# Layer 0 of a graph network: results turned over in pieces of four transposes, and the LSTM's output product cut in two

## The chip, the cores and the metric

The kernel runs on one NeuronCore of a Trainium2 chip. The metric is device time in microseconds (us), the median of several runs. One execution was also taken by the hardware profiler; its trace gives the start, length, tiles and releaser of each instruction. The engines are TensorE (PE; its weight loads are listed apart as PEld), VectorE (DVE), ScalarE (ACT), GpSimd (POOL) and SyncE (SP), which here only issues DMAs.

## The reference, cut to what matters

The input x holds 128 graphs of 64 nodes with 256 features, or 8192 tokens. Four layers follow one another, each x = x + f(relu(layernorm(x))). Layers 1 to 3 are an edge-softmax attention, a graph convolution with batch norms and a dense attention. The change lies in layer 0, with its last pieces of work in the first steps of layer 1:

```python
h = relu(einsum('ts,bsh->bth', adj, x @ Wg0 + bg0))
h = relu(einsum('ts,bsh->bth', adj, h @ Wg1 + bg1))
for p in range(1, 5):
    nw = 64 // p
    wins = h[:, :nw * p].reshape(128 * nw, p, 256)
    last = lstm_last(Wih[p-1], Whh[p-1], bih[p-1] + bhh[p-1], wins)
    h = h.at[:, arange(nw) * p + p - 1].set(last.reshape(128, nw, 256))
```

The LSTM starts from zero. At each of its p steps the gates i, f, g and o come from x_t @ Wih.T + h @ Whh.T + bias; then c = sigmoid(f)*c + sigmoid(i)*tanh(g) and h = sigmoid(o)*tanh(c). The last h overwrites the p-th node of each window, and the next p reads what the previous one left. All is in fp32.

## The kernel before, in words

**Where the data is.** The tokens are cut into 16 chunks of 512 and 4 groups of 2048. The features of a group lie transposed (256 features as 2 x 128 partitions, tokens along the free axis) in a tile hT. Only two such tiles fit, so the stage works in two halves: first groups 0 and 1, then groups 2 and 3. The features of groups 2 and 3 wait in device memory (hm8 to hm15) until a result of the first half has left hT.

**Steps.** A Step (L671) is one time step t of one window length w for one part of a group: 512 tokens wide for w=1, 256 for w=2, 336 for w=3, 256 for w=4. Each half runs w=1 to 4; the parts go in pairs whose steps alternate, so a state's next step comes a whole step of the other state later. Step.prepare (L693) makes the operand tile xop from hT: for w=1 by DVE (L704, L708 and the next), for larger w by copies L715 and L716 and subtractions L717, L723 and L724, on ACT and DVE, or on GpSimd where the first step of the other state stands beside it.

**Products.** The 256-deep product of a gate is done with seven products of 128x128 blocks, after Strassen and Winograd (L734 for all of them). Step.gate (L769) is a generator in four parts: products 1 and 2 (into PSUM tiles pa and pb; copy L777, add L778); products 6 and 7 (copies L782, L785); product 5 (add L788); products 3 and 4 (add L793), after which gate_done runs. The values of a gate lie in a tile of four blocks, numbered 0 to 3. Blocks 0 and 2 have feature half 0, blocks 1 and 3 half 1. Two activations (func, L762) finish the halves in the last part: the one of half 0 after product 3, the one of half 1 after product 4's add.

**gate_done** (L797) makes c (L811 to L814) and tanh(c) (L815). After gate o it makes the result: in the last step one product o*tanh(c) written straight into hT (L828), in earlier steps one product into a tile lstm_h (L833), and behind it three differences (L835 to L837) that the next step's products need. For w=1 it is two products per feature half (L820).

**The order is written by hand.** The loop over slots begins one gate per slot and keeps three in flight: the new gate's products 1 and 2, the oldest gate's 3 and 4 with gate_done, the middle gate's 5, the new gate's 6 and 7. At the end of the slot come the outputs that are due, preparing of the next step, loads of residuals (fetch_x, L855), and weights of later phases (L494, with sums on GpSimd at L506). Engines take their instructions in this order.

**PSUM.** In this stage the tag "bank" has two buffers. Product 2's pb and the transposes of results share them.

**Outputs.** group_out(g, c) (L862) returns chunk column c of a finished group: for each u of two, chunk n = 4g+2u+c, it calls add_transposed twice. Each call is four 128x128 transposes (L188) into one bank and one DVE add (L193) of the bank to the residual tile xres. After both calls GpSimd issues the store of xres to xa (L869). In the first half SP then issues the load (L872) that fills the freed columns of hT with those of the second half. A group is put out by two calls of 16 transposes, one slot and then three slots after its last step (two in the second half). xres has four buffers; loads for the next group stand later on SP's queue and wait for those stores. The last group's calls come in layer 1, one in each of the first two calls of edges (L1409); layer 1 has transposes of its own (L173), and adds L1070.

Of the kernel before, what the change touches and what calls it, by code (L numbers as in the profile page):

```python
# [31 lines left out]
def gnn_stack_kernel(ctx: ExitStack, tc: tile.TileContext, a: dict, out: bass.AP):  # L32
# [446 lines left out]
    with ExitStack() as l0:  # L479
# [191 lines left out]
        class Step:  # L671
# [97 lines left out]
            def gate(self, q):  # L769

                N = self.N
                pa = psl.tile([P, 512], F32, tag="pa", name="pa", bufs=3)
                pb = psl.tile([P, 512], F32, tag="bank", name="pb", bufs=2)
                pc = psl.tile([P, 512], F32, tag="pc", name="pc", bufs=3)
                self.product(q, ((1, pa, True), (2, pb, True)))
                blk, second = self.new_gate(q)
                nc.scalar.copy(blk[0, 0], pa[:, :N])  # L777
                nc.vector.tensor_tensor(blk[0, 0], pb[:, :N], blk[0, 0], ALU.add)  # L778
                self.func(q, blk[0, 0], blk[0, 0], 0)
                yield  # L780
                self.product(q, ((6, pa, False),))
                nc.scalar.copy(blk[1, 0], pa[:, :N])  # L782
                self.product(q, ((7, pc, True),))

                (nc.vector.tensor_copy if not self.t and self.w > 1 else nc.scalar.copy)(blk[1, 1], pc[:, :N])  # L785
                yield
                self.product(q, ((5, pa, False),))
                nc.vector.tensor_tensor(blk[1, 1], pa[:, :N], blk[1, 1], ALU.add)  # L788
                yield
                self.product(q, ((3, pa, False),))  # L790
                self.func(q, blk[0, 1], pa[:, :N], 0)
                self.product(q, ((4, pc, False),))
                nc.vector.tensor_tensor(blk[1, 0], pc[:, :N], blk[1, 0], ALU.add)  # L793
                self.func(q, second, second, 1)
                self.gate_done(q)

            def gate_done(self, q):  # L797
                N, state, t = self.N, self.state, self.t
                last = t == self.w - 1
                act = self.act  # L800
                if q == 2 and t:
                    for i_, g_ in zip(act[0], act[2]):
                        nc.vector.tensor_tensor(i_, i_, g_, ALU.mult)
                if (q == 1) if t else (q == 2):
                    if not t and self.w > 1:
                        state["c"] = [cp.tile([P, 4 * NMAX], F32, tag="c", name="lstm_c")[:, : 4 * N]]
                    for k in range(len(act[0])):
                        i_, g_ = act[0][k], act[2][k]
                        c_ = state["c"][k] if self.w > 1 else i_
                        if t:  # L810
                            nc.vector.tensor_tensor(act[1][k], act[1][k], c_, ALU.mult)  # L811
                            nc.vector.tensor_tensor(c_, act[1][k], i_, ALU.add)
                        else:
                            nc.vector.tensor_tensor(c_, i_, g_, ALU.mult)  # L814
                        nc.scalar.activation(g_, c_, AF.Tanh)  # L815
                if q != 3:
                    return
                if self.w == 1:
                    for j in range(2):
                        nc.vector.tensor_tensor(  # L820
                            self.nodes(slice(j, j + 3, 2), 0),
                            act[3][j].rearrange("p (u n) -> p u n", n=N),
                            act[2][j].rearrange("p (u n) -> p u n", n=N),
                            ALU.mult,
                        )
                elif last:
                    o_, g_ = (act[k][0].rearrange("p (q n) -> p q n", n=N) for k in (3, 2))
                    nc.vector.tensor_tensor(  # L828
                        self.nodes(slice(0, 4), t), self.as_nodes(o_), self.as_nodes(g_), ALU.mult
                    )  # L830
                else:
                    h = hop.tile([P, 7 * NMAX], F32, tag="h", name="lstm_h")
                    nc.vector.tensor_tensor(h[:, : 4 * N], act[3][0], act[2][0], ALU.mult)  # L833
                    v = h[:, : 7 * N].rearrange("p (q n) -> p q n", n=N)
                    nc.vector.tensor_tensor(v[:, 4:6], v[:, 2:4], v[:, 0:3:2], ALU.subtract)  # L835
                    nc.vector.tensor_tensor(v[:, 6], v[:, 3], v[:, 4], ALU.subtract)
                    nc.vector.tensor_tensor(v[:, 2], v[:, 1], v[:, 6], ALU.subtract)  # L837
                    state["h"] = {1: v[:, 0], 2: v[:, 1], 3: v[:, 3], 4: v[:, 2], 5: v[:, 4], 6: v[:, 6], 7: v[:, 5]}
# [20 lines left out]

        residual = {}  # L860

        def group_out(g, c):  # L862

            for u in range(2):
                n = 4 * g + 2 * u + c
                xt = residual.pop(n)
                for ip in range(2):
                    add_transposed(xt, 2 * ip, hTs0[g % 2][:, u], c * CHUNK + ip * 256)
                nc.gpsimd.dma_start(out=xa[n], in_=xt)  # L869
                if g < 2:  # L870
                    m = n + NCH // 2
                    nc.sync.dma_start(  # L872
                        out=hTs0[g][:, u, :, c * CHUNK : (c + 1) * CHUNK], in_=hmem[m]
                    )

        def first_norms1(norms):

# [25 lines left out]
        for slot in range(len(tasks) + 2):  # L903
# [13 lines left out]
            if len(flight) > 1:  # L917
                old = flight.pop(0)
                next(old[1], None)
                next(flight[-1][1])  # L920
            elif flight and not new:
                old = flight.pop(0)
                next(old[1], None)
            else:
                old = None
                if flight:
                    next(flight[-1][1])
            if new:
                next(one)
                flight.append((new, one))  # L930
                at, k = new[0], new[2]
                while outs and outs[0][0] <= slot:
                    group_out(*outs.pop(0)[1:])

                new_half = at + 1 < len(steps) and at and steps[at + 1].w == 1 < step.w
                if k == len(step.gates) - (1 if new_half else 2) and at + 1 < len(steps):
                    steps[at + 1].prepare(step)
                if step.w == MAX_SKIP and step.t == 2 and k < 2 and step.g < NGR - 1:
                    for u in range(2):
                        n = 4 * step.g + 2 * u + k  # L940
                        later.append((slot, "x", n))
# [7 lines left out]
            if old:  # L949
                (at, q, k), step = old[0], steps[old[0][0]]  # L950
                if k == len(step.gates) - 1:
                    if at + 1 == len(steps) or steps[at + 1].phase != step.phase:
                        phase_over(step.phase)
                    if step.phase == len(phases) - 1 and step.t == 1 and step.g == NGR - 1:

                        t_ = wsp.tile([P, 2, 4, 2, P], F32, tag="wih", name="x_first", bufs=2)
                        flat = t_.rearrange("p k q j m -> p k (q j m)")
                        norms1 = {}
                        for n in range(2):
                            xt = flat[:, n, :].rearrange("p (i d) -> p i d", i=4)  # L960
                            nc.sync.dma_start(out=xt, in_=xa[n])
                            norms1[n] = Norm(xt)
                        norm_steps = first_norms1(norms1)
                    if step.w == MAX_SKIP and step.t == MAX_SKIP - 1:
                        outs += [(slot + 1, step.g, 0), (slot + (3 if step.g < NGR // 2 else 2), step.g, 1)]
        last_outs = [(g, c) for _, g, c in outs]
    psums["banks"] = None


# [1 line left out]
    with ExitStack() as l1:  # L971
# [29 lines left out]
        nc.sync.dma_start(out=wlv[:, :, QS:], in_=a["W_valT"])  # L1001
        wout = w1.tile([P, 2, D], F32, tag="wout", name="wout")
        nc.sync.dma_start(out=wout, in_=a["W_outT"])
        for g, c in last_outs:
            for u in range(2):
                n = 4 * g + 2 * u + c
                residual[n] = fetch_x(n)

# [393 lines left out]
        def next_score():  # L1402
            q, lrs = waiting.pop(0)
            score(q, lrs)
            if q % 8 == 7:
                linear_part(q // 8)
                behind.append(edge_softmax(q // 8))

        def edges(q):  # L1409

            n, odd = q // 2, q % 2
            it = 2 * q
            halves = gather(it)
            if it + 2 < NT:
                project(it + 2)
            lrs = [joined(halves)]
# [5 lines left out]
            elif n + 2 < NCH:  # L1422
                for k in (2, 3):
                    norms1[n + 2].placed(k)
            if last_outs:
                group_out(*last_outs.pop(0))
            step_behind()
            halves = gather(it + 1)
            if it + 3 < NT:
                project(it + 3)  # L1430
            lrs.append(joined(halves))
# [784 lines left out]
```

## Time and profile before

| what | us |
|---|---|
| median of 3 runs | 1985.58 (1983.38 to 1989.72) |
| the profiled execution, its own time | 1985.91 |
| its span in the profile | 1984.1 |
| TensorE busy in it | 1938.8 |
| LSTM stage, about 190 to 1265: TensorE busy of 1075 | 1059.8 |
| the same: DVE, ACT, GpSimd busy | 643.7, 627.4, 146.5 |
| layer 1, about 1265 to 1540: TensorE busy of 275 | 265.1 |

The mean granted TensorE clock is 0.997 of full speed. A row of the timeline gives start, duration, engine, line, operation, tiles out<-in, shape, count, and in brackets the idle time ahead of it with what ended it. A row of the waits gives the engine, the tile and line that waited, what it waited for, and then us in total, times, and the longest. SPq is SP's queue of DMA issues. In the timeline the second half of the LSTM stage begins at about 700.

### The profile page before, as it was taken

What the parts mean: (1) busy time and instruction counts of PE and PEld (TensorE: products, weight loads), DVE (VectorE), ACT (ScalarE), POOL (GpSimd) and SP (SyncE); (2) the same over time, 40 slices, a digit from 0 to 9 for tenths busy, and PEclk for the clock granted to TensorE, in tenths of its full rate; (3) what the DMA queues carried; (4) which work ended last, traced back from release to release, by engine and by line L of the source; (5) the groups of instructions that cost most, each with busy time, mean ns of one, the idle gap of its engine ahead of it and who ended that gap; (6) DMA issues with size and microseconds to landing.
All of it is one profiled execution on the core that took longest, in us unless ns stands there. A gap on an engine that the chain in (4) does not pass through costs nothing. (4 is left out here: it accounts for less than half of the span.)

```text
span 1984.1 us, 25549 instructions
## 1 busy us (share of the span) xinstructions
PE 1938.8 (98%) x9406; PEld 1392.2 (70%) x9406; DVE 1309.4 (66%) x2454; ACT 1143.5 (58%) x2153; POOL 448.0 (23%) x590
## 2 busy tenths in 40 slices
PE   9999999999999999999999999999999999999998
PEld 7777478866678864788666788766556675534787
DVE  8774675575475557765654655657657777796886
ACT  4343775565465547665654656466666556593554
POOL 3000032030030011320300200255664430000574
PEclk9999999999999999999999999999999999999999
DMA  7522000010010054000100100441332842022112
GB/s 267 173 67 88 0 22 1 1 43 0 1 43 1 1 160 137 22 1 1 43 0 1 43 1 17 143 155 64 112 122 90 328 179 65 0 64 85 43 65 86
DMA packets 63869, 135.60 MB, mean 68 GB/s; under 512 B 6656, under 2 KB 41344, under 8 KB 61440
## 3 DMA queue, kind: packets, MB, share of 16 engines
q1 hardware_dynamic: 59808, 124.33, 18.4%
q0 software_dynamic: 3328, 9.44, 1.2%
q8 instruction: 74, 1.21, 0.3%
q14 instruction: 51, 0.42, 0.1%
q10 hardware_dynamic: 608, 0.20, 0.1%
HBM read 87.55 MB, written 46.40 MB: 68 GB/s over the span
## 5 line engine op out<-in xcount | busy, mean ns | idle before, releaser
L762 ACT ACTIVATE gate<-gate,bias 128x256 f32<-128x256 f32 (+2 forms) x368 | 247.1, 678 | 181.0 <-DVE gate L778 101.1
L734 PE MATMUL pa<-xop,sih 128*128 128x256 f32 (+2 forms) x1056 | 343.0, 418 | 6.7 <-DVE gate L788 6.4
L734 PEld LDWEIGHTS pa<-xop,sih 128*128 128x128 f32 x1056 | 199.2, 190 | 80.8 <-issue 20.1
L734 PE MATMUL pc<-xop,wih 128*128 128x256 f32 (+2 forms) x736 | 251.3, 423 | 0.0
L778 DVE TENSOR_TENSOR gate<-pb,gate 128x256 f32<-128x256 f32 (+2 forms) x184 | 87.4, 475 | 225.7 <-PE pb L734 150.4
L734 PE MATMUL pa<-lstm_h,shh 128*128 128x256 f32 (+1 forms) x672 | 212.8, 398 | 0.0
L734 PEld LDWEIGHTS pc<-xop,wih 128*128 128x128 f32 x736 | 140.1, 190 | 51.0 <-issue 22.4
L1102 ACT ACTIVATE lr<-pair 128x1024 f32<-128x1024 f32 x128 | 124.0, 1021 | 70.8 <-PE pair L1092 40.4
L793 DVE TENSOR_TENSOR gate<-pc,gate 128x256 f32<-128x256 f32 (+2 forms) x184 | 87.6, 476 | 112.0 <-PE pc L734 111.8
L734 PEld LDWEIGHTS pa<-lstm_h,shh 128*128 128x128 f32 x672 | 128.0, 190 | 29.9
L734 PE MATMUL pc<-lstm_h,whh 128*128 128x256 f32 (+1 forms) x448 | 141.9, 398 | 0.0
L777 ACT COPY gate<-pa 128x256 f32<-128x256 f32 (+2 forms) x184 | 75.9, 412 | 94.1 <-PE pa L734 93.6
L1061 PE MATMUL bank<-wlv,hT 128*128 128x260 f32 x480 | 122.3, 398 | 0.0
L788 DVE TENSOR_TENSOR gate<-pa,gate 128x256 f32<-128x256 f32 (+2 forms) x184 | 87.5, 476 | 43.5 <-PE pa L734 42.9
L762 ACT ACTIVATE gate<-pa,bias 128x256 f32<-128x256 f32 (+2 forms) x184 | 93.7, 509 | 29.4 <-PE pa L734 28.0
L1061 PEld LDWEIGHTS bank<-wlv,hT 128*128 128x128 f32 x480 | 87.5, 192 | 32.7 <-issue 15.3
L782 ACT COPY gate<-pa 128x256 f32<-128x256 f32 (+2 forms) x184 | 75.0, 407 | 52.6 <-PE pa L734 51.6
L734 PE MATMUL pa<-xop,wih 128*128 128x256 f32 (+1 forms) x320 | 101.7, 400 | 2.8 <-ACT xop L715 2.6
L734 PE MATMUL pb<-xop,wih 128*128 128x256 f32 (+1 forms) x320 | 100.5, 398 | 0.0
L734 PEld LDWEIGHTS pc<-lstm_h,whh 128*128 128x128 f32 x448 | 85.3, 190 | 19.9
L506 POOL TENSOR_TENSOR shh<-whh 128x512 f32<-128x512 f32 x6 | 8.1, 1355 | 385.4 <-DMA whh<-in_WhhT 385.4
L785 ACT COPY gate<-pc 128x256 f32<-128x256 f32 (+2 forms) x136 | 57.8, 425 | 52.6 <-PE pc L734 51.9
(376 smaller groups left out, 3964.1 us busy)
## 6 DMA issues: line engine op xcount, KB each, us to landing
field<-keep SPq DMA_DIRECT2D x4, 2304.0 KB, 14.4
wih<-in_WihT SPq DMA_DIRECT2D x8, 1024.0 KB, 7.0
xres<-in_x SPq DMA_DIRECT2D x16, 512.0 KB, 4.6
xa<-xres POOLq DMA_DIRECT2D x16, 512.0 KB, 4.9
dense<-field SPq DMA_DIRECT2D x4, 2048.0 KB, 8.9
xin<-xb SPq DMA_DIRECT2D x16, 512.0 KB, 3.8
h<-xb SPq DMA_DIRECT2D x16, 512.0 KB, 3.5
xin<-in_x SPq DMA_DIRECT2D x15, 512.0 KB, 5.9
```

The lines of the kernel that those rows point to most:

```text
L506: keep(nc.gpsimd.tensor_tensor(o, x, y, op))
L734: ins = nc.tensor.matmul(p[:, : self.N], weights[kind, self.phase](k, q), x[k], start=first_ and kind == "ih", stop=kind == "hh" or not se ...
L762: nc.scalar.activation(out, in_, AF.Tanh if q == 2 else AF.Sigmoid, bias=bias[:, self.w - 1, 2 * q + j : 2 * q + j + 1],)
L777: nc.scalar.copy(blk[0, 0], pa[:, :N])
L778: nc.vector.tensor_tensor(blk[0, 0], pb[:, :N], blk[0, 0], ALU.add)
L782: nc.scalar.copy(blk[1, 0], pa[:, :N])
L785: (nc.vector.tensor_copy if not self.t and self.w > 1 else nc.scalar.copy)(blk[1, 1], pc[:, :N])
L788: nc.vector.tensor_tensor(blk[1, 1], pa[:, :N], blk[1, 1], ALU.add)
L793: nc.vector.tensor_tensor(blk[1, 0], pc[:, :N], blk[1, 0], ALU.add)
L1061: ins = nc.tensor.matmul(o, hTs[n][:, k, i * P : (i + 1) * P], wlv[:, k, cols], start=k == 0, stop=k == 1)
L1102: nc.scalar.activation(lr, p, AF.Relu)
```

## The change: what it does

1. `group_out` returns one piece: four transposes, one add; with the second piece of a chunk go the store and, in the first half, the load of hT. A new function `some_out` puts out one due piece per call in the first half of the tasks and up to two per call later. It is called twice in each slot: between products 4 and 5, and where the calls stood before. All eight pieces of a group become due one slot after its last step.
2. What is left for layer 1 is put out by `last_out`, two pieces at each of two places in `edges`.
3. For w>1 a new method `hidden` makes the product o*tanh(c) in two halves of blocks: blocks 0 and 2 after the activation of half 0, ahead of product 4's add, and blocks 1 and 3 after the activation of half 1. The three differences of lstm_h stay behind the second half.

On SP's queue this turns the order around the first half's outputs from "load of hT, load of hT, residual, residual" into "load of hT, residual, load of hT, residual".

```diff
@@ gate @@
                 self.product(q, ((3, pa, False),))
                 self.func(q, blk[0, 1], pa[:, :N], 0)
+                if q == 3 and self.w > 1:
+                    self.hidden(slice(0, 3, 2))
                 self.product(q, ((4, pc, False),))
                 nc.vector.tensor_tensor(blk[1, 0], pc[:, :N], blk[1, 0], ALU.add)
                 self.func(q, second, second, 1)
+                if q == 3 and self.w > 1:
+                    self.hidden(slice(1, 4, 2))
                 self.gate_done(q)
+
+            def hidden(self, blocks):
+
+                N = self.N
+                o_, g_ = (self.act[k][0].rearrange("p (q n) -> p q n", n=N)[:, blocks] for k in (3, 2))
+                if self.t == self.w - 1:
+                    nc.vector.tensor_tensor(
+                        self.nodes(blocks, self.t), self.as_nodes(o_), self.as_nodes(g_), ALU.mult
+                    )
+                    return
+                if not blocks.start:
+                    self.h = hop.tile([P, 7 * NMAX], F32, tag="h", name="lstm_h")
+                v = self.h[:, : 7 * N].rearrange("p (q n) -> p q n", n=N)
+                nc.vector.tensor_tensor(v[:, blocks], o_, g_, ALU.mult)
@@ gate_done @@
-                elif last:
-                    o_, g_ = (act[k][0].rearrange("p (q n) -> p q n", n=N) for k in (3, 2))
-                    nc.vector.tensor_tensor(
-                        self.nodes(slice(0, 4), t), self.as_nodes(o_), self.as_nodes(g_), ALU.mult
-                    )
-                else:
-                    h = hop.tile([P, 7 * NMAX], F32, tag="h", name="lstm_h")
-                    nc.vector.tensor_tensor(h[:, : 4 * N], act[3][0], act[2][0], ALU.mult)
-                    v = h[:, : 7 * N].rearrange("p (q n) -> p q n", n=N)
+                elif not last:
+                    v = self.h[:, : 7 * N].rearrange("p (q n) -> p q n", n=N)
@@ outputs @@
-        def group_out(g, c):
-
-            for u in range(2):
-                n = 4 * g + 2 * u + c
-                xt = residual.pop(n)
-                for ip in range(2):
-                    add_transposed(xt, 2 * ip, hTs0[g % 2][:, u], c * CHUNK + ip * 256)
+        def group_out(g, c, u, ip):
+
+            n = 4 * g + 2 * u + c
+            xt = residual[n]
+            add_transposed(xt, 2 * ip, hTs0[g % 2][:, u], c * CHUNK + ip * 256)
+            if ip:
+                residual.pop(n)
                 nc.gpsimd.dma_start(out=xa[n], in_=xt)
                 if g < 2:
                     m = n + NCH // 2
                     nc.sync.dma_start(
                         out=hTs0[g][:, u, :, c * CHUNK : (c + 1) * CHUNK], in_=hmem[m]
                     )
+
+        def some_out(slot):
+
+            for _ in range(2 if slot > len(tasks) // 2 else 1):
+                if outs and outs[0][0] <= slot:
+                    group_out(*outs.pop(0)[1:])
@@ slots @@
                 next(old[1], None)
+                if new:
+                    some_out(slot)
                 next(flight[-1][1])
...
-                while outs and outs[0][0] <= slot:
-                    group_out(*outs.pop(0)[1:])
+                some_out(slot)
...
-                        outs += [(slot + 1, step.g, 0), (slot + (3 if step.g < NGR // 2 else 2), step.g, 1)]
-        last_outs = [(g, c) for _, g, c in outs]
+                        outs += [(slot + 1, step.g, c, u, ip) for c in range(2) for u in range(2) for ip in range(2)]
+        last_outs = [out[1:] for out in outs]
@@ layer 1 @@
+        def last_out():
+
+            for _ in range(2):
+                if last_outs:
+                    group_out(*last_outs.pop(0))
+
         def edges(q):
...
             halves = gather(it)
+            last_out()
...
-            if last_outs:
-                group_out(*last_outs.pop(0))
             step_behind()
             halves = gather(it + 1)
+            last_out()
```

More of the change, by code (lines that the diff above doesn't have):

```diff
@@ L1003, in gnn_stack_kernel @@
         nc.sync.dma_start(out=wout, in_=a["W_outT"])
-        for g, c in last_outs:
-            for u in range(2):
+        for g, c, u, ip in last_outs:
+            if not ip:
                 n = 4 * g + 2 * u + c
```

## The prediction, made before the changed kernel had run

> **What bounds the kernel now.** I read the page from the top: busy shares, then who keeps TensorE waiting, then the places.
>
> ```profile
> PE 1938.8 (98%) x9406; PEld 1392.2 (70%) x9406; DVE 1309.4 (66%) x2454; ACT 1143.5 (58%) x2153; POOL 448.0 (23%) x590
> ```
>
> TensorE is busy 98% of the 1984.1 us span. Only 45 us are waits, and the change takes no matmul away. TensorE's waits (us in total, times, longest) show what it can reach:
>
> ```profile
> PE bank L188 <- DVE xres L193: 6.9, 9, 2.3
> PE pa L734 <- DVE gate L788: 6.4, 10, 1.2
> ...
> PE pa L734 <- ACT xop L715: 2.6, 2, 1.3
> ```
>
> The first line is the transposes of results: 16 in a row through two banks, each freed by an L193 add. The other two are LSTM products that wait where phases meet. TensorE's timeline has the dearest place (start, duration, idle before):
>
> ```profile
> 720.88 1.04 PE L188 MATMUL bank<-ident,hT 128*128 128x128 f32 x8
> 724.25 1.25 PE L188 MATMUL bank<-ident,hT 128*128 128x128 f32 x8 [2.34 <-DVE xres L193]
> 725.34 1.81 PE L734 MATMUL pa<-hT,wih 128*128 128x512 f32 x2
> ```
>
> The last row does two products in 1.81 us that take 1.02 at 714.20: half clock. The table by windows says the same (PE, PEld, DVE, ACT, POOL busy; then granted clock, DMA share, GB/s):
>
> ```profile
> 725.00:729.00 4.00, 4.00 (x10) 1.92 (x10) 1.27 (x3) 0.58 (x1) 1.06 (x2) 0.57 0.75 215
> 729.00:733.00 4.00, 4.00 (x14) 2.45 (x13) 3.16 (x5) 1.99 (x4) 0.00 (x0) 1.00 1.07 365
> ```
>
> So a gap cost its own length and about 1.6 us of slow products behind it.
>
> **Part 1: the transposes.** Four transposes issue in 0.437 us (16 in 1.75). Issue gaps are the shown idle plus about 0.17, because matmul ends are modelled. What the rows of before lose to groups of 16:
>
> - first half, 705 to 757 (A): 0.73 (705.66 to 708.13 less 1.75), 0.6 for the product at 716.47 behind the late reload, 2.72 and 1.6 of clock (720.88 to 728.65), 0.73 (739.07), 2.18 (753.6 to 757.49). Sum 8.6 with rounding.
> - second half's first group, 1247 to 1260 (B): 0.73 and 1.29, together 2.0; the last group, inside layer 1 at 1273 to 1286: 1.6 and 1.15, together 2.75.
>
> After, four transposes stand between products of at least 0.86 us, and an L193 takes 0.69. One piece finds its bank long free. A pair fills both banks; the first L193 ends 0.44+0.1+0.69 = 1.23 us after its start, before the next products 2 begin at 0.87+0.86 = 1.73. So the bank waits go, where DVE comes at once.
>
> B: 0.73 of the first 2.0 stays, as the last pieces still meet L173's transposes (1258.89), so 1.3 is gained. Of layer 1's 2.75 some 0.2 stays, 2.5 gained; halving L828 (2.05 at 1267.46) frees the L1070 add that TensorE waits for at 1269.82, 0.4 by 0.59 shown. **B gains 4.1**, bounds 2 (only the waits shown, half of them) to 4.5.
>
> A has a price: the reload of the second half's features into hT (L872, on SP). Its rows on DVE, and on SP the longest wait of a residual load:
>
> ```profile
> 714.52 1.23 DVE L704 TENSOR_TENSOR xop<-hT 128x1024 f32<-128x1024 f32 x1 [3.94 <-DMA hT<-hm]
> ```
> ```profile
> SPq L855 <- DMA xa<-xres: 65.2, 12, 32.1
> ```
>
> Before, SP issues both reloads of a chunk (706.77, 708.36) and then the residual loads (713.74), which wait for the store of xa to land so that a buffer is free. After, the order is reload, residual load, reload, residual load: the second reload stands behind a load that waits for a store, and its own fourth piece comes only at about 713.65. The store would start at about 706.9 and land by 712 (stores here took 2.9, 4.9, 8.5), so the piece decides. Reloads took 4.0 to 6.0; 5.0 puts the landing at 718.65. Then L704 1.23, L793 0.42, L708 0.69 lead to 720.85 (adjacent DVE rows overlap a little), while TensorE would be at that product at 718.19: **a stall of 2.65** (1.65 to 3.65). It leaves an idle of about the length that halved the clock, so I add 1.6. The second chunk's second reload, issued at about 731.7, lands at 736 to 739; its L704 sits on DVE ahead of the L193 of a pair, so transposes wait 2.0 (0.7 to 3.5), and the products behind the pairs 1.5 and 0.8. After: 2.65+1.6+2.0+1.5+0.8 = 8.55, with 0.15 of small waits 8.7, against 8.6. But the sum by slots is kinder: followed slot by slot, the slot that starts at 757.49 starts at about 756, since some of these waits fall into time that TensorE's queue of ready products covers. **A gains 1.5**; bounds a loss of 5.6 (stalls 3.65 and 3.5, the dip twice, 2.3 of pb, 1.5 more behind the late adds) and a gain of 8.6 (reload in time).
>
> On the clock the Trainium skill speaks for the change. "TensorE: Matmul & The Clock Gate", "HAM oscillation — how this bites in real kernels", gives the rule that TensorE must not idle more than about 3.4 us. By it a stall of 2.65 costs no clock, and the sum would be 1.6 better; the row above, with an issue gap of 2.5 us followed by 3.3 us at half clock, decides against the rule.
>
> **Part 2: the split product.** 44 products become 88. A 128x1024 takes 1.23 (L704), a 128x512 0.69 (L708): 2x0.69-1.23 = 0.15 more per product, 6.6 us of DVE in all. DVE is busy about 55% in this stage, and in most steps h is needed a whole step (some 24 us) later, so both this and any gain are hidden there; if that cover were gone, 6.6 us would be the price. What counts is where phases meet, in pairs of like places of the two halves:
>
> ```profile
> 414.93 3.33 DVE L833 TENSOR_TENSOR lstm_h<-gate 128x1344 f32<-128x1344 f32 x1
> ```
> ```profile
> 556.96 0.70 PE L734 MATMUL pa<-xop,wih 128*128 128x256 f32 x2 [1.32 <-ACT xop L715]
> ...
> 570.44 0.70 PE L734 MATMUL pa<-xop,sih 128*128 128x256 f32 x2 [1.20 <-DVE gate L788]
> ```
>
> - w=2 to 3 (407.37, 0.40 idle): L828's chain ends 0.45 sooner; +0.9 for two.
> - w=3, first step (421.34, 0.66 idle): L833 took 3.33 beside GpSimd's sums L717 and L723 (1.55 for the same size at L811 alone). In the changed order all three lstm_h differences (1.15, 0.78, 1.15) stand ahead of adds that TensorE waits for. I take 0.7 later (0 to 1.3): -1.4 for two.
> - w=3 to 4 (556.96): TensorE waits for the copy L715 of ACT, it for L828 (553.74, 2.02). Half of it runs before the second activation, so its end comes about 1.0 sooner, ACT's 0.75: +1.5 for two.
> - w=4, first step (570.44): first half of h done before product 4's add; 0.43 sooner: +0.9 for two.
>
> **C gains 1.9**, bounds a loss of 0.5 and a gain of 4 (all of the waits at 556.96 and 570.44 gone, twice, less 1). One rule of the skill speaks against it: "SBUF — State Buffer", "SBUF: two separate sides", says that a DVE operation with two SBUF inputs and a GpSimd operation that reads SBUF exclude each other, the loser waiting for the whole instruction. By it each half could wait once: with L717's 2.33 us a second time the loss would be some 2 us at each of two places. The row 3.33 against 1.55 fits one such wait; none shows two, and I keep 0.7.
>
> **Sum.** The profiled run took 1985.91, 1.8 more than its span and 0.3 over the median of 1985.58. 1985.9-1.5-4.1-1.9 = **1978.4**; I take 1978.5. Against the median it would be 1978.1.
>
> **Rivals.**
> 1. *The reload eats it: slower.* The store of xa lands 8.5 us after issue (as one did), at 715.4; the load behind it holds SP, the reload starts at 715.6 and lands 6.0 later at 721.6: stall 5.6 and 1.6 of clock. The second chunk the same, 5.6 and 1.6, and 2.3 at the banks: 16.7 against 8.6, or 8.1 lost. B at its lower bound gives 2, C loses 0.5: 6.6 lost, 1992.5. It decides from a landing later than 715.9 (718.19 less the 2.3 of DVE); every us behind that is a us, and the sign turns once A loses what B and C bring. For: both reloads of before already arrive late (idle 3.94). Against: stores were mostly faster.
> 2. *Full cover.* Every bank wait goes and the reload comes in time or its wait is hidden by products that are ready: A 8.6, B 4.5, C 1.9: 15.0, so 1970.9. For: three gates in flight. Against: one reload cannot be issued before its piece at 713.65.
> 3. *Nothing moves.* The bank wait goes over to products 2, which share the two banks, and to the reload; A loses 3, B gives 3, C 0: 1985.9. For: DVE has L704, L828 and four L193 in the same 15 us. Against: single pieces have 4 us each.
>
> **Numbers.** Forecast, with part gains (1974 to 1982): 0.50. Rival 2: 0.12. Rival 3 (1982 to 1988): 0.24. Rival 1: 0.14. About 0.3%, 6.0 us, is what a measurement can tell from no change: faster means under 1979.6. Of the forecast about three quarters (0.37) lie below that, with rival 2 0.49; the rest of it (0.13) and rival 3 0.37; slower 0.14. The range leaves out about 0.1 at each end: 1972 to 1988.
>
> **What would show it.** Right: no wait of L188 for L193 over 1 us outside 730 to 745; the last slot of A about 1.5 us sooner; layer 1's L188 without idle; an idle of 2 to 3 us near 718 ended by DVE's L708, with half clock behind it; 556.96's wait below 0.7. Wrong: no idle near 718 (reload hidden, rival 2), or one over 4 us (rival 1); waits for L778's bank in place of L188's (rival 3); L833's halves summing to more than 4 us beside GpSimd.

## The result, and the profile after

The changed kernel took 1991.89 us (median of 8 runs, 1989.01 to 1995.02) against 1985.57 for the kernel before (8 runs, 1983.38 to 1990.12). The ratio is 1.003, 95% interval 1.002 to 1.004: about 6 us slower, where 7.4 us of gain was forecast. The profiled execution has a span of 1989.9 us at a clock of 0.995 (1984.1 and 0.997 before). Lines behind the edits are shifted: the add of product 4 is now L795, the halves of the product are L813 (into lstm_h) and L806 (into hT), its three differences are L846 to L848, the load of hT is L883, the residual load L866.

TensorE's waits after (us in total, times, longest):

```profile
PE pa L734 <- DVE gate L788: 11.0, 10, 2.1
PE pa L734 <- DVE xop L708: 5.2, 1, 5.2
...
PE bank L188 <- DVE xres L193: 2.3, 2, 1.9
...
PE pa L734 <- ACT xop L715: 1.2, 2, 0.7
```

The first part did what it was made for: the waits of the transposes fell from 6.9 to 2.3 us. The copy L715 fell from 2.6 to 1.2. But one wait of 5.2 us is new, and the waits for L788 rose from 6.4 to 11.0 with as many places.

The products L734 come in the same order in both traces, so the n-th of one can be set beside the n-th of the other. After minus before, in us:

| product that before starts at | after minus before | what lies between |
|---|---|---|
| 190.4 | -0.3 | |
| 280.9 / 348 / 421.3 | +0.9 / +1.3 / +2.6 | first steps of w=2 and w=3 |
| 557 | +1.9 | w=3 to w=4 |
| 757.5 | +5.7 | region A: +3.8 |
| 965.5 | +10.1 | first steps again, half clock at the last |
| 1098.5 | +9.5 | w=3 to w=4 |
| 1114.1 | +12.0 | first step of w=4, half clock |
| 1295 to 1400 (layer 1) | +7.5 | region B: -4.5 |
| end | +5.7 | before was at half clock for longer near 1473 |

So A lost 3.8, B gained 4.5, and the phase boundaries (C) lost 8.5: 2.2 in the first half and 6.3 in the second.

**A.** TensorE's timeline after:

```profile
719.68 0.59 PE L734 MATMUL pa<-lstm_h,shh 128*128 128x256 f32 x2
725.43 2.05 PE L734 MATMUL pa<-xop,sih 128*128 128x512 f32 x2 [5.15 <-DVE xop L708]
727.27 1.92 PE L734 MATMUL pc<-xop,wih 128*128 128x512 f32 x2
```

The wait runs back along L708 and L704 to the load of hT. SP's queue and DVE show why it is late:

```profile
708.69 0.57 SPq L883 DMA_DIRECT2D hT<-hm  x1
716.17 0.38 SPq L866 DMA_DIRECT2D xres<-in_x  x1
716.66 0.53 SPq L883 DMA_DIRECT2D hT<-hm  x1
```
```profile
723.12 1.23 DVE L704 TENSOR_TENSOR xop<-hT 128x1024 f32<-128x1024 f32 x1 [5.08 <-DMA hT<-hm]
```

The residual load between the two reloads waited until 716.17 for the store of xa that GpSimd had begun at 709.65, 6.5 us. Only then was the second reload issued, 1.7 us behind the start of its last transposes (714.93), and it landed 6.4 us later, with that residual load and another store of xa (716.57) under way beside it. The table by windows shows the price behind it; the seventh number is the granted clock:

```profile
725.40:729.20 3.80, 3.77 (x6) 1.63 (x7) 3.69 (x5) 0.63 (x2) 0.00 (x0) 0.50 0.01 4
746.30:750.50 4.20, 3.82 (x8) 1.52 (x9) 2.94 (x5) 0.59 (x1) 1.11 (x2) 0.60 1.01 363
```

The second row is the second chunk: 1.94 us of wait for an L193 that DVE reached only after the late L704, and half clock again.

**C.** The first step of w=2, VectorE before and after:

```profile
276.92 1.63 DVE L833 TENSOR_TENSOR lstm_h<-gate 128x1024 f32<-128x1024 f32 x1 [0.30 <-ACT gate L762]
```
```profile
275.68 2.05 DVE L813 TENSOR_TENSOR lstm_h<-gate 128x512 f32<-128x512 f32 x1
277.65 0.41 DVE L785 COPY gate<-pc 128x256 f32<-128x256 f32 x1
277.98 0.88 DVE L813 TENSOR_TENSOR lstm_h<-gate 128x512 f32<-128x512 f32 x1
```

The whole took 1.63 us; the halves took 2.05 and 0.88, where 0.69 each had been expected. GpSimd's L717 began at 275.67, just ahead of the first half, and took 1.51. TensorE, which waited for nothing there before, now waits 1.21 us for L788, and 2.06 in place of 0.66 at 423.94:

```profile
281.80 0.70 PE L734 MATMUL pa<-xop,sih 128*128 128x256 f32 x2 [1.21 <-DVE gate L788]
```

**B.** Late transposes of the last group inside layer 1, before and after:

```profile
1285.15 0.66 PE L188 MATMUL bank<-ident,hT 128*128 128x128 f32 x4 [0.84 <-DVE xres L193]
```
```profile
1285.75 1.09 PE L188 MATMUL bank<-ident,hT 128*128 128x128 f32 x8
```

### The profile page after: what moved, and what is told of

It is laid out like the page before. It is cut to its first block, busy times and chain, and to the rows that moved or that the text cites. A ratio compares the mean times of both kernels' runs of the same rounds, so it can differ in the third digit from the quotient of the medians.

```text
span 1989.9 us, 25607 instructions
## 1 busy us (share of the span) xinstructions
PE 1940.7 (98%) x9406; PEld 1392.2 (70%) x9406; DVE 1320.4 (66%) x2498; ACT 1147.7 (58%) x2153; POOL 443.3 (22%) x590
## 3 DMA queue, kind: packets, MB, share of 16 engines
q8 instruction: 74, 1.21, 0.3%
## 5 line engine op out<-in xcount | busy, mean ns | idle before, releaser
L734 PE MATMUL pa<-xop,sih 128*128 128x256 f32 (+2 forms) x1056 | 346.1, 421 | 16.4 <-DVE gate L788 11.0
L734 PEld LDWEIGHTS pa<-xop,sih 128*128 128x128 f32 x1056 | 199.4, 191 | 89.6 <-issue 26.8
L734 PE MATMUL pc<-xop,wih 128*128 128x256 f32 (+2 forms) x736 | 252.8, 425 | 0.0
L734 PE MATMUL pa<-lstm_h,shh 128*128 128x256 f32 (+1 forms) x672 | 213.1, 399 | 0.0
L734 PEld LDWEIGHTS pc<-xop,wih 128*128 128x128 f32 x736 | 140.5, 191 | 52.0 <-issue 23.3
L795 DVE TENSOR_TENSOR gate<-pc,gate 128x256 f32<-128x256 f32 (+2 forms) x184 | 87.7, 477 | 121.1 <-PE pc L734 120.7
L734 PEld LDWEIGHTS pa<-lstm_h,shh 128*128 128x128 f32 x672 | 128.1, 191 | 30.5 <-issue 0.4
L734 PE MATMUL pc<-lstm_h,whh 128*128 128x256 f32 (+1 forms) x448 | 141.8, 398 | 0.0
L788 DVE TENSOR_TENSOR gate<-pa,gate 128x256 f32<-128x256 f32 (+2 forms) x184 | 87.5, 476 | 41.6 <-PE pa L734 41.3
L734 PE MATMUL pa<-xop,wih 128*128 128x256 f32 (+1 forms) x320 | 101.6, 399 | 1.8 <-ACT xop L715 1.2
L734 PE MATMUL pb<-xop,wih 128*128 128x256 f32 (+1 forms) x320 | 100.5, 398 | 0.0
L734 PEld LDWEIGHTS pc<-lstm_h,whh 128*128 128x128 f32 x448 | 85.1, 190 | 20.1
L506 POOL TENSOR_TENSOR shh<-whh 128x512 f32<-128x512 f32 x6 | 7.6, 1272 | 386.8 <-DMA whh<-in_WhhT 252.7
L785 ACT COPY gate<-pc 128x256 f32<-128x256 f32 (+2 forms) x136 | 57.8, 425 | 52.5 <-PE pc L734 52.4
```

Of the source, the lines that this page charges most:

```text
L734: ins = nc.tensor.matmul(p[:, : self.N], weights[kind, self.phase](k, q), x[k], start=first_ and kind == "ih", stop=kind == "hh" or not se ...
```

## The experiments

Two theories first. Theory 1: the change has two separate losses, the reload in A and the split at the first steps, against the gain in B. Theory 2: the loss is the reload and the half clock it leaves, and the split is free. Ratios are to the kernel before, measured beside it on the same chip; the medians of before were 1984.58 (e1 to e4), 1986.75 (e5 to e8), 1987.09 (e9 to e12), 1986.90 (e13).

**e1, the pieces without the split.**

```diff
-                if q == 3 and self.w > 1:
-                    self.hidden(slice(0, 3, 2))
...
-                    self.hidden(slice(1, 4, 2))
+                    self.hidden(slice(0, 4))
```

> The pieces of four transposes as changed, the LSTM product whole as before. Theory 1 (two separate losses: the late reload of hT, about 3.8 us between 703 and 760, and the split first halves of lstm_h held up beside GpSimd's sums, 5 to 8 us over the phase boundaries; against them 4.5 us gained at the end of the stage): -0.7 us against before, between -3 and +1.5, and the phase boundaries at 281, 421 and 963 look as before. Theory 2 (the whole loss is the reload and the half clock it leaves, the split is free): as slow as the changed kernel, +5 to +7 us.

Measured 1983.90, ratio 0.9996 (0.9987 to 1.0005). By products A lost 3.2 and B gained 3.9, and the boundaries at 281, 421 and 963 look as before, to 0.1 us. Theory 1 holds, and theory 2 falls.

**e2, the split without the pieces**: `hidden` in the kernel before.

> The product o*tanh(c) in two halves as changed, the transposes 16 in a row as before. Theory 1: +5 to +8 us against before; TensorE waits for L788 of 1.2 us near 281 and 2 us near 421, which before had none and 0.66. Theory 2: -2 to 0 us, no wait of over 1 us for L788 at 281 and 421.

Measured 1993.35, ratio 1.0042 (1.0025 to 1.0059), about +8.3. The waits for L788 are even more than in the changed kernel:

```profile
PE pa L734 <- DVE gate L788: 14.3, 12, 2.2
PE bank L188 <- DVE xres L193: 6.9, 9, 2.3
```

So the split is the larger loss by far, and the pieces alone break even.

**e3, the pieces with group 1's residual loads later**, kept in program order behind group 0's first reloads.

```diff
-                        later.append((slot, "x", n))
+                        later.append((slot + 12 if step.g == 1 else slot, "x", n))
...
-            if n >= NCH - NCH // 4:
+            if n >= NCH - NCH // 4 or 4 <= n < 8:
                 late(ins)
```

> As the pieces alone, but the loads of residuals for group 1 stand on SP's queue behind the first three reloads of hT. If it is the queue (the load that waits for a store) that makes the second reload late: it is issued at about 715 in place of 716.7, lands 1.5 to 2 us sooner, the stall before the product of L708 shrinks from 5.15 to 3 to 3.7 us, and the time is 1 to 3 us under that of the pieces alone. If it is the place of the fourth piece alone: no change.

Measured 1980.53, ratio 0.9974 (0.9965 to 0.9983). TensorE's wait in that place is 1.96 us at 720.23 (5.36 at 723.46 in e1), less than the 3 expected, and the clock is 1.00 from 718 to 724. The time is 3.4 us under e1 by the medians and 4.4 by the ratios, more than expected; by products A gains 1.1 where e1 lost 3.2. So the residual loads on SP's queue are the cause of A's loss, and in two ways. L704 behind the second reload, in e1 and in e3:

```profile
721.15 1.23 DVE L704 TENSOR_TENSOR xop<-hT 128x1024 f32<-128x1024 f32 x1 [5.28 <-DMA hT<-hm]
```
```profile
717.93 1.22 DVE L704 TENSOR_TENSOR xop<-hT 128x1024 f32<-128x1024 f32 x1 [1.88 <-DMA hT<-hm]
```

The reload was issued at 714.59 in e1 and at 713.60 in e3, only 1.0 us sooner. But L704 started on it 4.3 us after issue in place of 6.6: with no residual load beside it, it landed 2.2 us faster. That is the larger share, and the expectation had reckoned with the wait in the queue alone. A wait of 3.14 us that DVE ends at 736.53 is left, with half clock behind it: L704 of the second chunk waits until 734.65 for a reload issued at 726.97, with other loads and stores under way.

**e4, two pieces per place from the start.**

```diff
-            for _ in range(2 if slot > len(tasks) // 2 else 1):
+            for _ in range(2):
```

> As the pieces alone, but two pieces per place from the start (the first half's outputs too). The fourth piece comes three places earlier, so the second reload is issued at about 709 to 710. If lateness of the reload is the whole loss between 703 and 760: the stall falls to under 1 us, no half clock there, and the time is 6 to 9 us under before. Rival, that pairs bring the bank waits back (two banks shared with pb): 2 to 4 us of waits for L193 there, time 3 to 5 us under before.

Measured 1974.91, ratio 0.9950 (0.9936 to 0.9964), 9.7 us under before by the medians and beyond the 6 to 9 expected. Both reloads of the first chunk are now issued ahead of the residual loads:

```profile
704.56 3.98 SPq L881 DMA_DIRECT2D hT<-hm  x2
710.00 5.75 SPq L864 DMA_DIRECT2D xres<-in_x  x2
```
```profile
716.34 1.25 PE L188 MATMUL bank<-ident,hT 128*128 128x128 f32 x8 [1.29 <-DVE xres L193]
719.00 1.12 PE L734 MATMUL pb<-hT,wih 128*128 128x512 f32 x2 [0.55 <-DVE xres L193]
```

Of the bank waits that pairs were to bring back, 1.29 and 0.55 us are left, and the clock is 1.00 from 690 to 770. The order that keeps TensorE's pieces smallest (singles) was the worse one, since a single is later.

**e5 and e6, the split without the pieces, only in some steps**: whole where t=0 (e5), halves only in the last step (e6).

```diff
+                halves = self.t                    # e6: self.t == self.w - 1
+                if q == 3 and self.w > 1 and halves:
+                    self.hidden(slice(0, 3, 2))
...
+                    self.hidden(slice(1, 4, 2) if halves else slice(0, 4))
```

> The transposes as before; the product in halves only in steps t>0, whole in the first step of each window length, where GpSimd prepares the other state's operand beside it. Theory 1 (the split costs only where GpSimd's sums stand beside it): the waits for L788 at 281 and 421 are as before (0 and 0.66), and the gains of the split in last steps are left: -2 to -4 us against before, some 11 us under the split alone. Theory 3 (the split costs everywhere, by 0.15 us of DVE each and by its place ahead of other adds): +2 to +6 us.

> The transposes as before; the product in halves only in the last step of each window, where it goes to hT (L828). Theory 1: -2 to -4 us against before, like the run before it, as inner steps t=1 and t=2 have neither gain nor loss. Theory 3: between 0 and the time of the run before it.

Measured 1985.27 and 1985.67, ratios 0.9996 (0.9987 to 1.0004) and 0.9997 (0.9989 to 1.0006). The 8.3 us are gone with the split of first steps: the cost lies there, not in the extra instructions as such. The expected 2 to 4 us of gain aren't there either, or not to be told from nothing; theory 1 was right in the place and wrong in this size.

**e7 and e8, without GpSimd's preparing**: the kernel before and the split alone, each with `apart = False`, so that ACT and DVE make those operands.

> The kernel before, but the operands that GpSimd prepares beside a first step are made by ACT and DVE as everywhere else. The base for the next run. DVE gets L717, L723 and L724 (1.06, 0.95 and less) at 6 pairs of places: +0 to +8 us against before.

> The split as changed, without GpSimd's preparing. Theory 1, if the two-input DVE product and GpSimd's sums exclude each other: the split costs at most 2 us over the run before it (or gains up to 4, from the last steps). If order and the extra instruction cost, not GpSimd: 6 to 9 us over the run before it, as with GpSimd (8.4).

Measured 1993.65 and 1998.79, ratios 1.0042 (1.0029 to 1.0055) and 1.0061 (1.0048 to 1.0074). By the ratios the split costs 3.8 us here, known to about 3.6, against 8.3 known to 3.4. The times alone don't settle it. The rows do. The halves in e8, in the first step of w=2:

```profile
276.84 0.68 DVE L813 TENSOR_TENSOR lstm_h<-gate 128x512 f32<-128x512 f32 x1
277.44 0.41 DVE L785 COPY gate<-pc 128x256 f32<-128x256 f32 x1
277.77 0.68 DVE L813 TENSOR_TENSOR lstm_h<-gate 128x512 f32<-128x512 f32 x1
```

0.68 each, the expected price, with nothing on GpSimd beside them. At 415.35 in e8, where GpSimd's weight sums (L506) have moved up beside the halves, the two take 3.65 again.

**e9, both halves behind the second activation.**

> The transposes as before; the product in two halves everywhere as changed, but both halves behind the second activation, where the whole product stood. If the early place of the first half (ahead of the product 4 add, beside GpSimd's L717) makes the loss: within 1.5 us of before. If it is that a product in two pieces meets GpSimd's sums twice: +3 to +8 us.

Measured 1996.37, ratio 1.0042 (1.0028 to 1.0057). It tells less than was meant: DVE's instructions at the first steps ran in the same order as in e2 (first half at 275.74, L785, second half at 278.06), as the first half needs the first activation alone and its place in the source doesn't hold it back. DVE's order is not everywhere that of the source: in the kernel before, too, L788 and L785 run at 275.65 and 276.19, ahead of L833 at 276.92, which stands earlier in the source.

**e13, the other cut**: blocks 0 and 1, then 2 and 3, both needing both activations, so that they stand where the whole product stood.

```diff
+                    self.hidden(slice(0, 2))
+                    self.hidden(slice(2, 4))
```

> The transposes as before; the product in two halves everywhere, but cut the other way (blocks 0 and 1, then 2 and 3), so that each half needs both activations and the two stand where the whole product stood, in an order that is otherwise that of before. If two pieces as such, each meeting GpSimd, make the loss of first steps: +6 to +9 us, and the pair takes over 2.5 us near 277 (the whole took 1.63). If the early start of a half that needs one activation only makes it (queued at the head of GpSimd's L717, and the later order behind it): within 2.5 us of before, no wait for L788 over 0.5 near 281, and the pair near 277 takes 1.6 to 2.2.

Measured 1994.26, ratio 1.0038 (1.0026 to 1.0051): the same loss with the early start taken away. The pair takes 2.24 us (between the two expectations), TensorE waits 1.20 us for L788 at 281.69 as in e2.

```profile
276.52 2.24 DVE L812 TENSOR_TENSOR lstm_h<-gate 128x512 f32<-128x512 f32 x2 [0.31 <-ACT gate L762]
```

What GpSimd does at this place, in the kernel before and in e13:

```profile
275.96 1.50 POOL L717 TENSOR_TENSOR xop<-hT 128x512 f32<-128x512 f32 x1
277.54 1.59 POOL L723 TENSOR_TENSOR xop<-xop 128x256 f32<-128x256 f32 x1
```
```profile
275.57 1.51 POOL L717 TENSOR_TENSOR xop<-hT 128x512 f32<-128x512 f32 x1
277.16 1.05 POOL L723 TENSOR_TENSOR xop<-xop 128x256 f32<-128x256 f32 x1
```

And DVE's next differences, before and e13:

```profile
279.94 0.61 DVE L836 TENSOR_TENSOR lstm_h<-lstm_h 128x256 f32<-128x256 f32 x1
```
```profile
280.15 1.15 DVE L846 TENSOR_TENSOR lstm_h<-lstm_h 128x256 f32<-128x256 f32 x1
```

Before, GpSimd's L723 took 1.59 us; when it began, the whole product was under way, until 278.55. In e13 it takes 1.05, and DVE pays: 2.24 for 1.63 in the product and 1.15 for 0.61 in the difference of the same size. The sum of the two is 1.15 us, the 1.16 by which the product of TensorE that waits for L788 is later. At the first step of w=3 the same: L723 from 2.11 to 1.39, the product from 3.33 to 4.12. The whole product had met L717 already (1.63, against 1.22 in e7 with nothing on GpSimd beside it), but L723 then waited for it. Cut in two, it lets L723 in between, and DVE waits for GpSimd a second time.

**e10 to e12, combinations**: pairs with the split in last steps (e10), pairs with the later residual loads (e11), all three (e12).

> Pieces in pairs from the start, and the product in halves in last steps only: -9.9 of the pairs and -1 of the split in last steps, so -10 to -12 us against before.

> Pieces in pairs from the start, product whole, residual loads of group 1 behind all reloads of group 0's columns. If SP's queue still costs in the pairs' order (the second chunk's reloads stand behind two loads that wait for a store): 1 to 2 us under the pairs. If the second chunk's reloads are early enough (L704 at 727.48 waited for TensorE, not for the load): no difference, -9 to -11 us.

> Pieces in pairs, residual loads behind the reloads, and the product in halves in last steps only: between -10 and -13 us against before, and not above the pairs with the split in last steps.

Measured 1976.16, 1976.95 and 1975.12, ratios 0.9944 (0.9930 to 0.9958), 0.9949 (0.9935 to 0.9963) and 0.9942 (0.9928 to 0.9956). None can be told from e4's 0.9950. For e11 that was the second of its two expectations: in the pairs' order the second chunk's reloads are early enough. The pairs alone, one number changed in the source and the split left out, beat the kernel before by about 10 us; nothing else here adds to it measurably.

## Why the prediction was wrong, step by step

- **What bounds the kernel**: right. Every gain and loss was a wait of TensorE, or half clock behind one.
- **B**: right, in mechanism and size. Forecast 4.1 gained (its parts add up to 4.2), 4.5 in the profile. The pieces alone give 3.9 of it (e1), and e2, with the split alone, gains 0.6 between 1262 and 1280, where halving L828 was to give 0.4. Layer 1's L188 stand there without idle.
- **A, the reload**: the mechanism was right, two terms were mis-sized. The changed kernel ran 1.9 us late at 690; on before's times the product was due at 718.2, as forecast, but the reload was issued at 714.7 and not at 713.65. The step said "the piece decides", with the store of xa taking at most 5.1 us and landing in time. It took 6.5, so the load behind it held SP. That is 1.1 of the loss. The reload then took 6.4, not 5.0, which is 1.4 more. Together they make the 5.15 of the stall out of the forecast 2.65. The rows of before, 8.5 and 6.0 at most, allowed both; the middle was taken.
- **A, the rest of the sum**: by the products' rows half clock cost some 2.4 us behind the first wait and 1.7 behind the second chunk's, where one dip of 1.6 was forecast; the waits at the second chunk themselves were smaller (1.94 and 0.38, where 2.0, 1.5 and 0.8 were forecast). The kinder slot count, 1.5, rested on ready products that hide part of the waits, and nothing hid the 5.15 us. "A gains 1.5" became a loss of 3.8 (3.2 in e1).
- **A, the clock**: right where the rule of the Trainium skill was weighed against the row. "TensorE: Matmul & The Clock Gate", "HAM oscillation — how this bites in real kernels", sets the point at idle gaps of about 3.4 us. Half clock followed idle times of 1.94 (746.30) and 2.07 (971.43), and it did not follow one of 2.06 (423.94). The traces show what decides. Leaving out the start and the end of a span, every stretch of half clock in the 15 traces is 3.41 or 6.83 us long, and within a trace they all begin on one grid of 3.41 us. What counts is TensorE's idle time inside one cell of that grid, in one wait or several. The 1.94 us lay within one cell (743.76 to 747.17); the 2.06 were cut by a border at 422.87 into 1.0 and 1.1. From 1119.24 to 1122.65 parts of three waits, the longest 1.44, add up to 2.0, and half clock followed. In the LSTM stage of all traces 16 cells at full clock had 1.94 us of idle or more by the profile, and half clock followed each of them; it followed one of 1.80 and not one of 1.86, and no other.
- **C**: the step that failed most. It forecast 1.9 gained; the changed kernel lost 8.5 there, and e2 8.3 in all. As it came, for the first and the second half: first step of w=2, 1.2 and 1.1 lost, and 0.4 each with the second pair of parts; first step of w=3, 1.4 lost each (0.7 forecast); w=3 to 4, 0.7 and 1.5 gained (1.5 forecast for two); first step of w=4, nothing and 3.3 lost (0.9 gain forecast for two); 407.37 and its like, 0.1 and nothing (0.9 gain forecast for two). About 3.4 us of the loss is half clock, one cell at the first step of w=3 and one at that of w=4, both in the second half; the forecast had no term for it. The price of the split was put at the first step of w=3 alone. The first step of w=2 was not in the list, because TensorE did not wait there before: where no wait stood there was no slack either.
- **C, the rule set aside**: "SBUF — State Buffer", "SBUF: two separate sides", says that a DVE operation with two SBUF inputs and a GpSimd operation that reads SBUF exclude each other, the later one waiting for the whole instruction. The prediction gave the price by it and kept its own 0.7, as "none shows two" such waits. Rows here agree with the page: a half took 2.05 beside L717 and 0.68 with nothing on GpSimd beside it, and L723 took 1.59 behind the whole product and 1.05 beside the halves.
- **The 0.15 us of DVE per product**: right to cost it at nothing away from the boundaries (e5, e6).
- **Rival 1** ended at 1992.5, near the 1991.89 measured, and its mechanism was there. But it put 8.1 of loss into A and 0.5 into C; measured were 3.8 and 8.5, with B at its better end, so that its total came so close is luck.

## What to carry to other kernels

Before a DVE operation is cut in pieces, look at what GpSimd does in the same microseconds: the pieces let GpSimd in between, and the wait changes sides, here to the engine on the critical path. When a store, a load that waits for it and another load share one queue, spreading the work out puts waiting loads ahead of urgent ones and lets them share the transfer (e3); keep the urgent ones together (e4), even where that makes larger pieces for the matmul engine. And a place without a wait in the profile isn't a place with slack.

## What the runs showed of the hardware that was not expected

An exclusion costs neither engine by itself: it is paid by the one that comes second, so cutting an operation on one engine made an instruction of the other faster (L723, 1.59 to 1.05 us, with nothing of its own changed). The same 512 KB reload took some 4.3 us to land with no residual load beside it (e3) and 6.6 with one (e1), and that weighed more than the 1.0 us it stood in the queue. Half clock came after 1.94 us of idle in one place and not after 2.06 in another, because the idle time counts by cells of a fixed 3.41 us grid: two shorter waits in one cell can cost the clock, and a longer one across a border need not. That e8's split still costs 3.8 us by the ratios (5.1 by the medians) is explained only in part, by the halves that met the weight sums at w=3.
